# Reordering the second layer of a two-layer image network: next-sample statistics, fractional mix, square roots, final chunks

## The chip, the cores and the metric

The kernel runs on one core of a Trainium2 chip. A core has five engines with a queue of instructions each: TensorE (PE) multiplies matrices from on-chip memory (SBUF) into accumulators (PSUM), VectorE (DVE), ScalarE (ACT) and GpSimd (POOL) work on vectors, and SyncE (SP) issues transfers (DMA). Each engine takes its instructions in the order of its queue and waits at the head of it until the input is there. The metric is the device time of one launch in microseconds (us), lower is better.

## The reference: what is computed

Two residual layers on a batch of 32 images of 96 channels x 56 x 56, each after a group norm over 3 channels:

```python
x = x + L0(_gn(x))      # 1x1 conv to 576 channels, quantise; depthwise 3x3, quantise; 1x1 conv back; + its input
x = x + L1(_gn(x))      # three branches of 32 channels, joined, then a 3x3 conv 96 -> 96

# L1, cut:
x_0, x_05, x_1 = (x[:, :C0], x[:, C0:C - C0], x[:, C - C0:])
x_0 = _group_conv(x_0, conv0_w[None] * Y0[..., None, None], conv0_b, 1)          # spatial branch, gated 3x3
alpha = ALPHA_MIN + (ALPHA_MAX - ALPHA_MIN) * sigmoid(_mlp(gap, ...))[:, 0]      # one angle per sample
Fre = _frft2d(x_05, _frft_mat(H, alpha), _frft_mat(W, alpha))                    # fractional branch
Mix = _group_conv(concat(Fre.real, Fre.imag), conv05_w[None] * Y..., conv05_b, 0)
IFRFT = jnp.abs(_frft2d(Fre_out, _frft_mat(H, -alpha), _frft_mat(W, -alpha))) / (H * W)
...                                                                              # Fourier branch for x_1
out = jnp.concatenate([x_0, IFRFT, x_1], axis=1)
out = conv3x3(out, conv2_w) + conv2_b
```

The gates Y0, Y, Y1 and alpha come from small networks on the channel means of the sample. The absolute value of the fractional branch is a sum of two squares and a square root.

## The kernel before: the parts that the change touches

A sample goes through layer 0 while the sample before it goes through layer 1. Each layer is a list of steps with a weight, and two lists are merged by their weights:

```python
def interleave(a, b):
    ta, tb = sum(c for c, _ in a) or 1, sum(c for c, _ in b) or 1
    ...                               # take from a while (done of a) / ta <= (done of b) / tb

for i in range(B):
    conv, nxt = now["conv"], None
    if i + 1 < B:
        nxt = layer0(i + 1)
        conv[8:8] = nxt["norm"]                       # statistics of the next sample
        at = 2 * (4 * NB - LEAD) + 1                  # NB = 5, LEAD = 7
        conv[at:at] = nxt["split"]                    # its normalised input in two parts
    interleave(conv, one[:-4])                        # one: layer 1 of the sample before
    interleave(now["last"], one[-4:-2])
    head, two, done = layer1(i)
    interleave(head + (nxt["first"] if nxt else []), one[-2:] + end)
    if i + 2 < B:
        load(i + 2)
    one, end, now = two, done, nxt
```

The program's text gives an order of emission; the order of each engine's queue is fixed when the kernel is built, `tile.TileContext(nc, schedule_with_timeline_sim=True)`. Buffers come from pools: `p2` holds two of each tile, `ps1` four PSUM banks, `ps0` two pairs of banks, `xp` three input images.

Layer 0. `expand` (the tiles pe) is the 1x1 convolution to 576 channels of one of four phases of the image; ScalarE and then VectorE quantise it into one of three q1s tiles, and SyncE sends it on to the tiles qp of `depthwise` (pd). `project` (pp) is the last convolution, added into x:

```python
def norm():
    for j in range(NCH):
        nc.vector.bn_stats(stats[:, j, :], xt[:, j * CN : (j + 1) * CN])   # line 333, tile bn
    mean, rstd, _ = group_stats(...)                                       # small matmuls pma, pva
    ...
def expand(b, k):
    ps = pair(...)
    ...                                                                    # 4 matmuls, vh and vl
    src = q1s[turn["q1s"] % 3]
    turn["q1s"] += 1
    quant_act(ps, A1[:, b : b + 1], B1[:, b : b + 1], src[:, :, :PH], ...)
    for g in range(n):
        nc.sync.dma_start(out=qps[(NB * i + b) % 3][...], in_=src[g * G : (g + 1) * G]...)

conv = []
for g in range(NG0):                                  # NG0 = 18
    conv += de[g : g + 1] + ex[LEAD + g : LEAD + g + 1]   # depthwise g, then an expansion
```

Layer 1. After the gates (sg) come `weights` (the gated weights g0, g1, g2), `angles` (cs, and vv by way of pj and pvv), then the branches. `mix_t` (px, tile PQ) and `hilbert` (pr) are the Fourier branch, `spatial` (ps) the first one. The fractional branch mixes its channels, goes through DRAM (z) to be turned, and comes back as zh, with rows of the image in partitions, and az:

```python
def mix_f(j):                                         # j = 0 .. 3
    if j == 0:
        s["z"] = dp.tile([128, 2, HH], F32, tag="z", ...)
    at = slice(HN * j, HN * (j + 1))                  # HN = 392
    for h in range(2):                                # half h of the image: partitions 64 h and on
        t = p2.tile([128, HN], F32, tag="zs", ...)
        rows = slice(LOW * h, LOW * h + G + 2)        # 34 rows
        ps = bank(ps1, f"pm{i}_{j}_{h}")
        nc.tensor.matmul(ps[:, :HN], g1[rows], s["xf"][rows, at], start=True, stop=True)
        if h:
            nc.vector.tensor_copy(t, ps[:, :HN])
        else:
            nc.scalar.copy(t, ps[:, :HN])
        nc.sync.dma_start(out=s["z"][:, h, at], in_=t)
    if j < 3:
        return
    ...                                               # 2 reads z -> zh, then 8 reads z -> az

def rows_f(g):      ...   # g = 0 .. 3: matmuls pi on zh, copies into Y
def columns_f(g):   ...   # g = 0 .. 3: matmuls pz on Y, + az, Square, sum of two -> Z; tile sq has the tag zs

def magnitude():
    dst = cat[G : 2 * G, 1 : 1 + H, 1 : 1 + W].rearrange("p (q r) w -> p q r w", r=4)
    for r in range(4):
        nc.scalar.activation(dst[:, :, r, :], s["Z"][G * r : G * (r + 1)], AF.Sqrt)

def final(j):                                         # j = 0 .. 6: 8 rows of the output each
    ...                                               # 9 matmuls pc on cat, added into x

first = [(0.5, means), (1.0, gates), (0.1, norm)]
steps = [(0.5, weights), (1.0, angles)] + each(1.1, mix_t, 4) + each(1.0, mix_f, 4)
sp = each(2.7, spatial, 2)
steps += sp[:1] + each(2.1, hilbert, 2) + each(1.3, rows_f, 4) + each(1.2, columns_f, 4)
steps += [(0.0, magnitude)] + sp[1:]
steps += each(6.7, final, NCH)                        # NCH = 7
```

`cat` holds the three branches with a border of one element, for the 3x3 convolution. After the last final, `store` writes x out, which frees the image's buffer for `load(i + 2)`.

Of the kernel before, what the change touches and what calls it, by code (L numbers as in the profile page):

```python
# [50 lines left out]
NB = 5  # L51
# [12 lines left out]
LEAD = 7  # L64
L = 57
# [38 lines left out]
def block_kernel(ctx: ExitStack, tc: tile.TileContext, out: bass.AP, a: dict):  # L104
# [8 lines left out]
    p3 = ctx.enter_context(tc.tile_pool(name="p3", bufs=3))  # L113
    dp = ctx.enter_context(tc.tile_pool(name="dp", bufs=2, space=bass.MemoryType.DRAM))
# [138 lines left out]
    for k in range(3):  # L253
        t = cp.tile([128, PH, PW], FP8, tag=f"q1s{k}", name=f"q1s{k}")
        nc.gpsimd.memset(t, 0.0)
        q1s.append(t)
# [68 lines left out]
    def layer0(i):  # L325
# [42 lines left out]
        def expand(b, k):  # L368
# [10 lines left out]
            src = q1s[turn["q1s"] % 3]  # L379
# [70 lines left out]
    def layer1(i):  # L450
# [193 lines left out]
        def mix_f(j):  # L644

            if j == 0:
                s["z"] = dp.tile([128, 2, HH], F32, tag="z", name=f"z{i}")
            at = slice(HN * j, HN * (j + 1))
            for h in range(2):
                t = p2.tile([128, HN], F32, tag="zs", name=f"zs{i}_{j}_{h}")  # L650
                rows = slice(LOW * h, LOW * h + G + 2)
                ps = bank(ps1, f"pm{i}_{j}_{h}")
                nc.tensor.matmul(ps[:, :HN], g1[rows], s["xf"][rows, at], start=True, stop=True)  # L653
                if h:
                    nc.vector.tensor_copy(t, ps[:, :HN])
                else:
                    nc.scalar.copy(t, ps[:, :HN])
                nc.sync.dma_start(out=s["z"][:, h, at], in_=t)
            if j < 3:
                return  # L660
            z = s["z"].rearrange("o u n -> o (u n)")
            for k in range(2):
                nc.sync.dma_start(
                    out=zh[LOW * k : LOW * k + W, :, :W], in_=z[G * k : G * (k + 1)].rearrange("o (h w) -> h o w", w=W)
                )
            az = p1.tile([128, H // 4, 2, W], F32, tag="az", name=f"az{i}")
            s["az"] = az
            for r in range(4):
                for t in range(2):
                    src = z[2 * G + G * t : 3 * G + G * t].rearrange("o (q r w) -> r o q w", r=4, w=W)  # L670
                    nc.sync.dma_start(out=az[G * r : G * (r + 1), :, t, :], in_=src[r])
# [22 lines left out]
        def columns_f(g):  # L694
# [15 lines left out]
            sq = p2.tile([128, 8 * W], F32, tag="zs", name=f"sq{i}_{g}")  # L710
# [6 lines left out]
        def magnitude():  # L717
            dst = cat[G : 2 * G, 1 : 1 + H, 1 : 1 + W].rearrange("p (q r) w -> p q r w", r=4)
            for r in range(4):
                nc.scalar.activation(dst[:, :, r, :], s["Z"][G * r : G * (r + 1)], AF.Sqrt)  # L720
# [252 lines left out]
```

## Time and profile before

| | |
|---|---|
| time, median of 3 runs | 4761.99 us (4741.11 to 4764.95) |
| profiled run | span 4750.5 us, mean granted TensorE clock 0.941 |
| TensorE busy | 4293.0 us, 90% |
| VectorE / ScalarE / GpSimd busy | 2393.3 / 2177.6 / 176.7 us |
| final matmuls pc, line 746 | 1620.7 us |
| depthwise pd, line 398 | 956.8 us |
| expansion pe, line 372 | 434.7 + 351.7 us |
| mix pm, line 653 | 202.7 us, 768 ns mean |
| q1s quantisation waiting for qp transfers | 82.6 us in all |

How to read it: a matmul of float32 data shows as two records, so 16 pm matmul records belong to 8 matmuls of a sample. A bracket after a timeline line tells how long the engine stood idle before it, and which engine, tile and line released it. In a table of stretches the columns are: length, busy time and number of instructions of PE, PEld (the weight load), DVE, ACT, POOL, then the granted TensorE clock (1.00 is full), the DMA engines' share, and GB/s. TensorE counts as busy when it works slowly.

### The profile page before, as it was taken

To read this page: it belongs to the slowest core of one execution; us is meant where nothing else is said; L and a number is where in the kernel's file an instruction comes from. 1 tells how busy PE (TensorE), PEld (TensorE's weight loads), DVE (VectorE), ACT (ScalarE), POOL (GpSimd) and SP (SyncE) were. 2 spreads that over 40 slices of the span, in tenths; PEclk is the share of its full clock that TensorE was granted. 3 is DMA by queue.
4 is the path that set the end of the run, shared out by engine and by line. 5 is a ranking of instruction groups with operands and counts; after the bars stand their busy time and mean duration, and the time that the engine had idled before them with its cause. 6 is when DMAs were issued, how large, how long until landed. Compare 5 with 4: busy or idle time off the path is not lost.

```text
span 4750.5 us, 59888 instructions
## 1 busy us (share of the span) xinstructions
PE 4293.0 (90%) x21632; PEld 2471.1 (52%) x21632; DVE 2393.3 (50%) x5385; ACT 2177.6 (46%) x2824; POOL 176.7 (4%) x209
## 2 busy tenths in 40 slices
PE   3799999999998999999999999999999999999987
PEld 2545555545555555555555555455555555555544
DVE  5545545545445455455454455454454554555532
ACT  3534445444455444455444454444454444554431
POOL 1000000000000000000000000000000000000000
PEclk9899999999999999999999999999999999999998
DMA  2212222211223211222211222122222112222112
GB/s 72 44 48 45 42 61 65 64 46 39 48 62 65 62 38 36 59 64 65 58 40 39 58 65 64 43 42 48 62 65 63 35 39 58 65 64 53 33 34 48
DMA packets 397243, 249.58 MB, mean 53 GB/s; under 512 B 283233, under 2 KB 390100, under 8 KB 390804
## 3 DMA queue, kind: packets, MB, share of 16 engines
q1 hardware_dynamic: 394368, 242.76, 23.0%
q8 instruction: 172, 2.82, 0.3%
q10 hardware_dynamic: 2580, 2.99, 0.2%
q14 instruction: 123, 1.01, 0.1%
HBM read 92.90 MB, written 89.92 MB: 38 GB/s over the span
## 4 chain that ended last, share of the span: by engine, by line
PE 63%; DVE 14%; DMA 11%; ACT 6%; issue 4%; SPq 3%; POOL 0%; DVEq 0%; ACTq 0%; POOLq 0%
PE pc L746 31%; PE pd L398 12%; PE pp L414 5%; DMA zh<-z 4%; PE pe L372 4%; PE pm L653 4%; DMA qp<-q1s 3%; PE pi L678 3%; ACT cat L720 2%; SPq L385 2%; DMA z<-zs 2%; DVE bn L333 2%; DVE q1s L315 2%; DVE x L426 2%; DMA x<-in_x_dram 1%
## 5 line engine op out<-in xcount | busy, mean ns | idle before, releaser
L746 PE MATMUL pc<-cat,wc 96*96 96x448 f32 x4032 | 1620.7, 557 | 60.9 <-ACT cat L720 60.9
L746 PEld LDWEIGHTS pc<-cat,wc 96*96 96x96 f32 x4032 | 664.1, 168 | 895.5 <-issue 809.0
L398 PE MATMUL pd<-qp,dw 128*128 128x392 fp8e4 x4608 | 956.8, 353 | 43.0 <-ACT qtd L313 37.9
L313 ACT ACTIVATE qtd<-pd,o,s 128x784 int16<-128x784 f32 x576 | 576.4, 1001 | 908.1 <-PE pd L398 878.2
L313 ACT ACTIVATE qte<-pe,o,s 128x784 int16<-128x784 f32 x640 | 635.9, 998 | 685.3 <-PE pe L372 669.5
L398 PEld LDWEIGHTS <-dw 128*128 128x128 fp8e4 x4608 | 447.4, 102 | 502.2 <-issue 203.9
L372 PE MATMUL pe<-vh,w1r 96*128 96x392 f32 x1280 | 434.7, 422 | 71.1 <-DVE x L426 41.2
L315 DVE TENSOR_SCALAR q1s<-qte 128x784 fp8e4<-128x784 int16 x640 | 358.8, 562 | 240.4 <-ACT qte L313 144.3
L315 DVE TENSOR_SCALAR q<-qtd 128x784 bf16<-128x784 int16 x576 | 207.0, 359 | 499.1 <-ACT qtd L313 496.4
L754 DVE SCALAR_TENSOR_TENSOR x<-pc,bc,x 96x448 f32<-96x448 f32 x224 | 152.0, 679 | 582.7 <-PE pc L746 581.2
L372 PE MATMUL pe<-vl,w1r 96*128 96x392 f32 x1280 | 351.7, 357 | 0.0
L372 PEld LDWEIGHTS pe<-vh,w1r 96*128 96x128 f32 x1280 | 221.8, 198 | 222.2 <-issue 94.9
L653 PE MATMUL pm<-xf,g 34*128 34x392 f32 x512 | 202.7, 768 | 107.5 <-DVE bn L333 105.0
L414 PE MATMUL pp<-q,w3q 32*96 32x392 bf16 x4608 | 255.8, 327 | 2.2 <-DVE x L426 2.2
L372 PEld LDWEIGHTS pe<-vl,w1r 96*128 96x128 f32 x1280 | 246.1, 198 | 0.5
L426 DVE SCALAR_TENSOR_TENSOR x<-pp,s,x 96x392 f32<-96x392 f32 x256 | 142.2, 616 | 175.8 <-PE pp L414 175.8
L414 PEld LDWEIGHTS <-w3q 32*96 32x96 bf16 x4608 | 182.0, 118 | 84.6 <-issue 31.5
L726 PE MATMUL ps<-xq,g 128*128 128x392 f32 x512 | 201.1, 536 | 0.0
L678 PE MATMUL pi<-cs,zh 120*120 120x112 f32 x1024 | 136.9, 295 | 63.8 <-DMA zh<-z 57.9
L333 DVE BATCH_NORM_STATS2 bn<-x 96x6 f32<-96x448 f32 x224 | 121.1, 608 | 133.6 <-DMA x<-in_x_dram 133.6
L361 ACT CAST vh<-v 96x392 fp32r<-96x392 f32 x256 | 126.2, 516 | 128.7 <-DVE v L353 127.9
L678 PEld LDWEIGHTS pi<-cs,zh 120*120 120x120 f32 x1024 | 131.6, 209 | 75.6 <-DVE cat L640 24.1
(149 smaller groups left out, 3881.5 us busy)
## 6 DMA issues: line engine op xcount, KB each, us to landing
qp<-q1s SPq DMA_DIRECT2D x2304, 26.2 KB
z<-zs SPq DMA_DIRECT2D x256, 196.0 KB
x<-in_x_dram SPq DMA_DIRECT2D x32, 1176.0 KB
out_dram<-x SPq DMA_DIRECT2D x32, 1176.0 KB
zh<-z SPq DMA_DIRECT2D x64, 392.0 KB
az<-z SPq DMA_DIRECT2D x256, 98.0 KB
xf<-vv SPq DMA_DIRECT2D x128, 6.1 KB
prep<-in_w_dram ACTq DMA_DIRECT2D x1, 864.0 KB
```

What stands on the lines that cost most here:

```text
L313: nc.scalar.activation(t.rearrange("p (h n) -> p h n", h=2), ps[:, :, :HN], AF.Relu, bias=offset, scale=scale)
L315: nc.vector.tensor_scalar(dst, src, 15.0, None, ALU.min, saturate=False if dst.dtype == FP8 else None)
L333: nc.vector.bn_stats(stats[:, j, :], xt[:, j * CN : (j + 1) * CN])
L372: nc.tensor.matmul(ps[:, h, :HN], w1[:, 128 * b : 128 * (b + 1)], v[:, k, HN * h : HN * (h + 1)], start=(n == 0), stop=(n == 1),)
L398: nc.tensor.matmul(ps[:, h, :HN], dw[:, g, t, :], view(qps[(NB * i + b) % 3][:, j, :], at, [[PW, PH // 2], [1, PH]]), start=(t == 0), stop ...
L414: nc.tensor.matmul(s["pp"][k // 2][:C, k % 2, :HN], w3[rows, g, :], s["q2"][rows, g, HN * h : HN * (h + 1)], start=(g == 0), stop=(g == NG ...
L426: nc.vector.scalar_tensor_tensor(part, src, A3, part, ALU.mult, ALU.add)
L653: nc.tensor.matmul(ps[:, :HN], g1[rows], s["xf"][rows, at], start=True, stop=True)
L678: nc.tensor.matmul(ps[: LOW + W, 2 * W * k : 2 * W * (k + 1)], zh[:, c : c + 2, :].rearrange("p c w -> p (c w)")[:, : LOW + W], cs, start= ...
L726: nc.tensor.matmul(ps[:, :HN], s["g0"][:, 128 * k : 128 * (k + 1)], view(xq, PH // 2 * h * (W + 2) + k, [[W + 2, PH // 2], [2, PH]]), star ...
L746: nc.tensor.matmul(ps[:C, :CN], wc[:, C * t : C * (t + 1)], cat[:, CR * j + dy : CR * j + dy + CR, dx : dx + W], start=(t == 0), stop=(t = ...
L754: nc.vector.scalar_tensor_tensor(part, ps[:C, :CN], bc, part, ALU.add, ALU.add)
```

## The change

It reorders layer 1 and its seam with layer 0: the next sample's statistics are emitted later; the fractional mix goes by image halves, so that the first half can be read back while the second is mixed, with four staging buffers instead of two; both spatial steps come before the Fourier branch's second part; the square roots are split by rows, so that the first final chunks need only the first part; four final chunks instead of two stand at the border between samples, as work that is ready while the gates are computed; five q1s tiles instead of three.

```diff
+NQ = 5
+HOLD = 4
+    p4 = ctx.enter_context(tc.tile_pool(name="p4", bufs=4))
-    for k in range(3):
+    for k in range(NQ):                              # q1s tiles
-            src = q1s[turn["q1s"] % 3]
+            src = q1s[turn["q1s"] % NQ]
...
-        def mix_f(j):                                # body before: above
+            if j == 0:                               # j = 0 .. 7
+                s["z"] = dp.tile([128, HW], F32, tag="z", name=f"z{i}")
+            h, k = divmod(j, 4)
+            rows = slice(LOW * h, LOW * h + G + 2)
+            ps = bank(ps1, f"pm{i}_{j}")
+            nc.tensor.matmul(ps[:, :HN], g1[rows], s["xf"][rows, HN * k : HN * (k + 1)], start=True, stop=True)
+            t = p4.tile([128, HN], F32, tag="zs", name=f"zs{i}_{j}")
+            if j % 2:
+                nc.vector.tensor_copy(t, ps[:, :HN])
+            else:
+                nc.scalar.copy(t, ps[:, :HN])
+            nc.sync.dma_start(out=s["z"][:, HN * j : HN * (j + 1)], in_=t)
+            if k < 3:
                 return
+            for t in range(2):
+                src = s["z"][G * t : G * (t + 1), HH * h : HH * (h + 1)].rearrange("o (h w) -> h o w", w=W)
+                nc.sync.dma_start(out=zh[LOW * t + PH * h : LOW * t + PH * (h + 1), :, :W], in_=src)
+            if h == 0:
+                return
             ...                                      # the 8 reads of az as before
-            sq = p2.tile([128, 8 * W], F32, tag="zs", name=f"sq{i}_{g}")
+            sq = p4.tile([128, 8 * W], F32, tag="zs", name=f"sq{i}_{g}")
-        def magnitude():
+        def magnitude(h):
+            at = slice(8 * h, min(8 * h + 8, H // 4))
             for r in range(4):
-                nc.scalar.activation(dst[:, :, r, :], s["Z"][G * r : G * (r + 1)], AF.Sqrt)
+                nc.scalar.activation(dst[:, at, r, :], s["Z"][G * r : G * (r + 1), at], AF.Sqrt)
...
-        steps = [(0.5, weights), (1.0, angles)] + each(1.1, mix_t, 4) + each(1.0, mix_f, 4)
-        sp = each(2.7, spatial, 2)
-        steps += sp[:1] + each(2.1, hilbert, 2) + each(1.3, rows_f, 4) + each(1.2, columns_f, 4)
-        steps += [(0.0, magnitude)] + sp[1:]
+        steps = [(1.0, angles), (0.5, weights)] + each(1.1, mix_t, 4) + each(0.6, mix_f, 8)
+        sp, co = each(2.7, spatial, 2), each(1.2, columns_f, 4)
+        steps += sp + each(2.1, hilbert, 2) + each(1.3, rows_f, 4)
+        for h in range(2):
+            steps += co[2 * h : 2 * h + 2] + [(0.1, lambda h=h: magnitude(h))]
         steps += each(6.7, final, NCH)
...
-            conv[8:8] = nxt["norm"]
-            at = 2 * (4 * NB - LEAD) + 1
+            at = 2 * (4 * NB - LEAD)
             conv[at:at] = nxt["split"]
+            conv[at - 6 : at - 6] = nxt["norm"]
-        interleave(conv, one[:-4])
-        interleave(now["last"], one[-4:-2])
+        interleave(conv, one[: -HOLD - 2])
+        interleave(now["last"], one[-HOLD - 2 : -HOLD])
-        interleave(head + (nxt["first"] if nxt else []), one[-2:] + end)
+        interleave(head + (nxt["first"] if nxt else []), one[-HOLD:] + end)
```

More of the change, by code (lines that the diff above doesn't have):

```diff
@@ L646, in mix_f @@
             if j == 0:
[L647 to L659, printed above, removed]
-                return
[L661 to L665, printed above, removed]
+                s["z"] = dp.tile([128, HW], F32, tag="z", name=f"z{i}")
[10 more added lines that the diff above has]
+            if k < 3:
+                return
+            for t in range(2):
[3 more added lines that the diff above has]
+                return
             az = p1.tile([128, H // 4, 2, W], F32, tag="az", name=f"az{i}")
@@ L669, in mix_f @@
                 for t in range(2):
-                    src = z[2 * G + G * t : 3 * G + G * t].rearrange("o (q r w) -> r o q w", r=4, w=W)
+                    src = s["z"][2 * G + G * t : 3 * G + G * t].rearrange("o (q r w) -> r o q w", r=4, w=W)
                     nc.sync.dma_start(out=az[G * r : G * (r + 1), :, t, :], in_=src[r])
```

## The prediction

> **What bounds the kernel now.** I read the page first, then who waits for TensorE's inputs in the steady part (288 to 4467 us, 29 samples of 144.1 us each), then the timeline around the largest wait, then the granted clock stage by stage. The page:
>
> ```profile
> PE 4293.0 (90%) x21632; PEld 2471.1 (52%) x21632; DVE 2393.3 (50%) x5385; ACT 2177.6 (46%) x2824; POOL 176.7 (4%) x209
> ...
> PEclk9899999999999999999999999999999999999998
> ```
>
> TensorE sets the time: 90% busy, the others at half. Only two things can shorten the run without touching the arithmetic: TensorE's idle time, and time at a reduced clock. The waits of TensorE (total us, times, longest) in the steady part:
>
> ```profile
> PE pm L653 <- DVE bn L333: 105.0, 29, 4.3
> PE pc L746 <- ACT cat L720: 48.8, 29, 2.0
> PE pi L678 <- DMA zh<-z: 46.1, 24, 3.9
> PE pe L372 <- DVE x L426: 40.0, 30, 1.3
> PE pmb L295 <- DVE mvb L293: 26.1, 29, 0.9
> PE pd L398 <- ACT qtd L313: 25.6, 58, 0.5
> PE pj L578 <- DVE de L576: 11.4, 29, 0.4
> ```
>
> Per sample (divide by 29): 3.6 us for the next sample's statistics, 1.7 for the square roots, 1.6 for the image read back from DRAM, 1.4 and 0.9 at the border, 0.9 and 0.4 around the angles. The first is the strange one, so the timeline of VectorE and TensorE there:
>
> ```profile
> 2050.99 0.27 DVE L599 COPY vv<-pvv 56x112 f32<-56x112 f32 x1
> 2055.85 3.78 DVE L333 BATCH_NORM_STATS2 bn<-x 96x6 f32<-96x448 f32 x7 [4.59 <-DMA x<-in_x_dram]
> 2059.56 0.73 DVE L622 COPY PQ<-px 112x256 f32<-112x256 f32 x2
> ```
>
> ```profile
> 2055.19 0.52 PE L372 MATMUL pe<-vl,w1r 96*128 96x392 f32 x2
> 2059.69 2.44 PE L653 MATMUL pm<-xf,g 34*128 34x392 f32 x4 [3.98 <-DVE bn L333]
> ```
>
> VectorE stands 4.59 us at a statistics instruction whose input is still being loaded, then spends 3.78 us on it; the copies that free TensorE's PSUM banks stand behind it in the queue. And what follows costs more than the gap (columns: length, busy times, granted clock, DMA share, GB/s):
>
> ```profile
> 2056.00:2060.00 4.00, 0.31 (x1) 0.30 (x2) 4.00 (x9) 0.93 (x2) 0.00 (x0) 1.00 0.03 6
> 2060.00:2067.00 7.00, 7.00 (x18) 2.64 (x17) 3.30 (x9) 1.95 (x3) 0.00 (x0) 0.50 0.26 84
> 2067.00:2074.00 7.00, 7.00 (x21) 2.71 (x20) 1.61 (x4) 2.52 (x4) 0.00 (x0) 0.52 0.38 130
> 2074.00:2088.00 14.00, 11.74 (x71) 8.81 (x71) 7.35 (x20) 8.55 (x12) 0.55 (x1) 1.00 0.74 117
> ```
>
> The 4 us gap is followed by 14 us at half clock. TensorE counts as busy there, so the 90% hides it. The trace holds its own experiment: sample 31 has no next sample, hence no such statistics. The same stretch, from the first matmul after the gates to the first final matmul, for sample 30 and for sample 31:
>
> ```profile
> 4348.30:4416.60 68.30, 57.62 (x312) 38.73 (x310) 35.47 (x93) 39.56 (x57) 0.55 (x1) 0.93 0.46 100
> 4492.30:4552.10 59.80, 52.87 (x297) 36.96 (x295) 29.68 (x75) 37.61 (x55) 0.00 (x0) 0.97 0.43 94
> ```
>
> 68.3 - 59.8 = 8.5 us: that is what a wholly removed statistics stall is worth per sample, gap and slow clock together.
>
> **What the Trainium skill says.** "TensorE: Matmul & The Clock Gate", section "What's actually happening": TensorE's clock falls to half after about one idle window of 3.4 us and comes back after about as much sustained work. The trace agrees on the fall (3.98 us idle, then 0.50); the way back takes 14 us here[...]. The 1.65 us gap before the final matmuls at 2105.83 brings no half clock, so only the largest gap matters for it. "TensorEngine Tiling (Array Packing)", section "Key Properties": tiles on different row groups can load and multiply in parallel. The trace agrees: in the mix (34 rows, at partition 0 and partition 64 in turn) two matmuls of 392 columns take 0.93 us at full clock (sample 31), while the 128-row spatial matmul of 392 columns takes 3.02 / 4 = 0.75 us for one. "ScalarE: Activation LUTs", section "What ACT_TABLE_LOAD costs": about 1283 ns a load; the page's row has 1283 ns, once per sample for Sqrt.
>
> **The change, part by part, per sample.** To place things I laid out the emission order by the weights of the interleaved lists, before and after.
>
> *Statistics later.* They are emitted ahead of the depthwise group 4 in the kernel before, and ahead of group 10, after rows_f(1), in the changed one. Counting TensorE work from the head of layer 1: old place 46 us after the head's start, new place about 84 (7 + 10 expansions at 0.95, 10 depthwise at 1.4, 4 finals at 7.0, the rest some 26). The load lands 44 us after the head's start now (2055.85 - 2011.9). It will land later, at some 54 to 58, because the store that frees its buffer comes after two more finals. In program order the wait would be gone with 26 us to spare. But the trace does not show program order: VectorE reaches bn right after vv, ahead of PQ copies that the program puts earlier, and sample 1's statistics ran at 15.68 us, long before their place. The order is fixed when the kernel is built (schedule_with_timeline_sim), by an estimate of when inputs are ready. So I give the full 8.5 us only half a chance: **-4.2**.
>
> *Mix by image halves, 4 buffers.* The same 8 matmuls, copies (485 and 564 ns) and writes. zh becomes 4 reads of half size instead of 2; the first pair goes out while half two is mixed. Now the chain from the last copy to the first row matmul is 0.57 + 2.66 (write) + 0.4 (issue) + 7.77 (read) = 11.4 us, against 11.2 us of TensorE work emitted between (one spatial, two expansions, two depthwise, hilbert 3.6). After: five expansions 4.7, five depthwise 7.0, two spatial 5.9, hilbert 3.6 = 21.2 us. The wait goes: **-1.6**. The price: matmuls that alternated between row groups now come four times from the same one. Alone each is at most 0.75 us, a pair 1.5 instead of 0.93, so up to 4 x 0.57 = 2.3 us; some neighbours will still overlap: **+1.5**. 4 zs buffers remove waits of the copies for z writes, which are not TensorE's; 5 q1s buffers likewise.
>
> *Square roots in two parts.* Four of 867 ns become four of 448 elements and four of 336. From Square (448: 577 ns, 224: 389) the slope is 0.84 ns an element, so 0.57 and 0.48 us: 4.2 us instead of 3.5 on ScalarE, which has room; the table load stays one. Half of it happens while columns are still computed. Of the 1.7 us wait: **-1.2**.
>
> *Four finals at the border.* The conv list keeps one final instead of three, the head has four instead of two: 14 us more filler between gates and mix_t, where TensorE now waits 0.4 for pj and 0.9 for qtd: **-0.9** of 1.3. The gaps before pe and pmb (2.3 us) lie ahead of the first final that can start; I leave them.
>
> Sum: -4.2 - 1.6 + 1.5 - 1.2 - 0.9 = -6.4 us per sample, x 29 = -186 us: 4762 - 186 = **4575 us**.
>
> **The rivals.** (1) *The stall stays and moves.* bn is again queued at the moment its load is thought to land, now amid mix_f; gap and half clock come back. For it: the two cases of reordering above. Then only -2.2 per sample remains, 64 us: about 4700. (2) *Everything works.* The stall goes wholly, -10.7 per sample, 310 us: about 4450; for it sample 31, and that the DVE has more other work ready at the new place. (3) *The row-group loss and new waits win.* +2.3 for the mix, a conv phase with only one final as ready filler while its chain of small steps is stretched, late loads pushing the statistics and the splits: +1 to +4 per sample, 4790 to 4880. Against it: TensorE's idle share is spread over waits that all get more filler.
>
> **Range and chances.** I weigh (2) at about a third (4420 to 4500), a stall that is shorter and no longer triggers the half clock at a third (4540 to 4660), (1) at a quarter (4670 to 4750), (3) at a tenth. 2% faster is 4667. Eight in ten: 4400 to 4780. Faster by over 2% 0.64, within 2% 0.27, slower 0.09.
>
> **What would show it.** The wait of pm (or any matmul) for bn gone or under 2 us, and mean granted clock up from 0.941 towards 0.97: the first step right; a wait of VectorE for x of 4 us or more: wrong. No wait of pi for zh. The pc wait for cat under 0.6 us. pm's mean up and its busy total per sample over 5 us: the row-group price. A new gap over 3.5 us anywhere, with half clock after it, would make the prediction wrong.

## The result, and the profile after

The changed kernel takes 4922.16 us in the median (4908.78 to 4942.46) against 4760.41 us of the kernel before in the same measurement: a ratio of 1.0351, 95% interval 1.0305 to 1.0398. It is 3.5% slower, where 4575 us and a gain were predicted, and it lies above the predicted range.

Per tile, TensorE's busy and idle time (idle is the time it stood just before the tile), in us of the whole profiled run:

| tile, what it is | before, busy / idle | after, busy / idle |
|---|---|---|
| pm, fractional mix | 202.7 / 107.5 | 244.7 / 106.7 |
| pc, final chunks | 1620.7 / 60.9 | 1706.3 / 82.4 |
| pd, depthwise | 956.8 / 43.0 | 950.9 / 84.6 |
| pe, expansion (vh and vl) | 786.4 / 71.1 | 838.7 / 67.1 |
| pp, projection | 255.8 / 2.2 | 291.7 / 35.3 |
| pi, rows of zh | 136.9 / 63.8 | 120.2 / 0.2 |
| pj, angles | 26.8 / 19.4 | 26.3 / 0.9 |
| TensorE at half clock, sum of the clock records | 566 | 796 |

From the page of the changed kernel, the busy times of its engines and the group of the mix matmuls (busy, mean ns | idle before them, and who ended it):

```profile
PE 4468.9 (91%) x21632; PEld 2622.8 (53%) x21632; DVE 2399.9 (49%) x5385; ACT 2192.9 (45%) x2952; POOL 188.1 (4%) x211
...
L654 PE MATMUL pm<-xf,g 34*128 34x392 f32 x512 | 244.7, 634 | 106.7 <-DMA qp<-q1s 46.8
```

The span grew by 172.7 us (4750.5 to 4923.2), TensorE's busy time by 175.9 for the same 21632 instructions. The idle time did not change (457.5 and 454.3 us); it is the same work that got slower. The mean granted clock fell from 0.941 to 0.919. Half clock grew by 230 us in the records, and half of that, 115 us, is time lost (an estimate from the two sums); the mix matmuls alone are busy 42 us longer. Who makes TensorE wait in the steady part (300 to 4650 us; total us, times, longest):

```profile
PE pc L749 <- ACT cat L723: 73.3, 29, 2.7
PE pd L401 <- ACT qtd L316: 67.7, 58, 1.6
PE pm L654 <- DMA qp<-q1s: 46.8, 13, 4.4
...
PE pm L654 <- DMA xf<-vv: 33.5, 9, 5.0
PE pp L417 <- DVE x L429: 32.0, 29, 1.1
...
PE pm L654 <- issue: 23.5, 7, 3.5
```

The wait of pi for zh is gone from the list, as the change meant. The wait of pm is still there, 103.8 us in three lines under three new names; the wait for the square roots grew from 48.8 to 73.3, that for qtd from 25.6 to 67.7, and the one ahead of the second projection is new. VectorE's own wait at the statistics in that part:

```profile
DVE bn L336 <- DMA x<-in_x_dram: 109.8, 29, 5.1
```

That is 3.8 us per sample: the statistics stand again at the head of VectorE's queue before their input is there. SyncE's issues, and then TensorE and VectorE, around it:

```profile
2132.52 0.83 SPq L606 DMA_DIRECT2D xf<-vv  x1
2133.47 0.79 SPq L133 DMA_DIRECT2D x<-in_x_dram  x1
2134.31 2.40 SPq L606 DMA_DIRECT2D xf<-vv  x3
```

```profile
2141.73 3.78 DVE L336 BATCH_NORM_STATS2 bn<-x 96x6 f32<-96x448 f32 x7 [4.00 <-DMA x<-in_x_dram]
2142.16 4.75 PE L654 MATMUL pm<-xf,g 34*128 34x392 f32 x8 [3.88 <-DMA qp<-q1s]
...
2150.43 2.90 PE L654 MATMUL pm<-xf,g 34*128 34x392 f32 x8
```

The load, 1176 KB, is issued between the four small transfers of vv (6.1 KB each) that the mix reads. It lands at 2141.73, and only then does the mix begin. The mix itself (16 records are 8 matmuls) takes 4.75 + 2.90 = 7.65 us. The stretches after the stall, and after the first final matmul (columns as in the prediction):

```profile
2142.00:2149.00 7.00, 6.84 (x15) 3.06 (x16) 5.54 (x12) 0.97 (x2) 0.00 (x0) 0.57 0.30 96
2149.00:2156.00 7.00, 7.00 (x23) 3.97 (x22) 1.98 (x4) 2.76 (x4) 0.00 (x0) 0.74 0.80 230
...
2186.70:2196.70 10.00, 10.00 (x22) 4.14 (x23) 1.80 (x4) 4.09 (x7) 0.00 (x0) 0.83 0.03 7
```

A stretch of low clock follows the square roots. In the kernel before, that was so in some samples only; two of them, ten microseconds from the first final matmul:

```profile
810.60:820.60 10.00, 9.95 (x22) 4.22 (x23) 8.31 (x18) 6.33 (x11) 0.00 (x0) 0.83 0.02 5
2105.83:2115.83 10.00, 10.00 (x27) 4.46 (x28) 8.98 (x19) 6.60 (x12) 0.00 (x0) 1.00 0.02 5
```

Counted over 28 samples, from the third to the thirtieth, half clock falls into these ten microseconds in 12 of 28 before and in 28 of 28 after. What stands ahead of them in the changed kernel (table load, square roots, first final matmuls):

```profile
2182.98 1.28 ACT L723 ACT_TABLE_LOAD   x1
...
2184.28 2.36 ACT L723 ACTIVATE cat<-Z 32x448 f32<-32x448 f32 x4
...
2186.69 4.16 PE L749 MATMUL pc<-cat,wc 96*96 96x448 f32 x6 [2.53 <-ACT cat L723]
```

The gap is 2.53 us, against 1.65 before, although this part of the square roots is shorter than the undivided ones (2.36 instead of 3.50 us).

### The profile page after: what moved, and what is told of

Read it like the earlier page. It is cut to its first block, busy times and chain, and to the rows that moved or that the text cites. A ratio compares the mean times of both kernels' runs of the same rounds, so it can differ in the third digit from the quotient of the medians.

```text
span 4923.2 us, 59961 instructions
## 1 busy us (share of the span) xinstructions
PE 4468.9 (91%) x21632; PEld 2622.8 (53%) x21632; DVE 2399.9 (49%) x5385; ACT 2192.9 (45%) x2952; POOL 188.1 (4%) x211
## 4 chain that ended last, share of the span: by engine, by line
PE 73%; DVE 14%; ACT 5%; issue 4%; DMA 3%; SPq 1%; POOL 0%; DVEq 0%; ACTq 0%; POOLq 0%
PE pc L749 32%; PE pd L401 12%; PE pe L375 7%; PE pp L417 6%; PE pm L654 5%; PE ps L729 4%; DVE vl L365 2%; DVE x L429 2%; PE px L619 2%; DVE v L356 2%; DVE Y L692 1%; ACT qte L316 1%; DMA xf<-vv 1%; ACT qtd L316 1%; DMA qp<-q1s 1%
## 5 line engine op out<-in xcount | busy, mean ns | idle before, releaser
L749 PE MATMUL pc<-cat,wc 96*96 96x448 f32 x4032 | 1706.3, 582 | 82.4 <-ACT cat L723 82.4
L749 PEld LDWEIGHTS pc<-cat,wc 96*96 96x96 f32 x4032 | 698.1, 176 | 972.1 <-issue 880.0
L401 PE MATMUL pd<-qp,dw 128*128 128x392 fp8e4 x4608 | 950.9, 354 | 84.6 <-ACT qtd L316 79.0
L375 PE MATMUL pe<-vh,w1r 96*128 96x392 f32 x1280 | 463.8, 447 | 67.1 <-DVE x L429 37.1
L375 PE MATMUL pe<-vl,w1r 96*128 96x392 f32 x1280 | 374.9, 377 | 0.0
L654 PE MATMUL pm<-xf,g 34*128 34x392 f32 x512 | 244.7, 634 | 106.7 <-DMA qp<-q1s 46.8
L375 PEld LDWEIGHTS pe<-vh,w1r 96*128 96x128 f32 x1280 | 250.0, 215 | 164.8 <-issue 84.4
L417 PE MATMUL pp<-q,w3q 32*96 32x392 bf16 x4608 | 291.7, 327 | 35.3 <-DVE x L429 35.3
L417 PEld LDWEIGHTS <-w3q 32*96 32x96 bf16 x4608 | 206.2, 117 | 120.2 <-DVE x L429 47.1
L654 PEld LDWEIGHTS pm<-xf,g 34*128 34x128 f32 x512 | 111.1, 228 | 201.7 <-issue 157.0
L336 DVE BATCH_NORM_STATS2 bn<-x 96x6 f32<-96x448 f32 x224 | 121.1, 608 | 120.2 <-DMA x<-in_x_dram 120.2
L741 DVE TENSOR_SCALAR cat<-ps,b 32x392 f32<-32x392 f32 x128 | 79.9, 624 | 139.9 <-ACT cat L743 139.9
```

The lines of the kernel that those rows point to most:

```text
L375: nc.tensor.matmul(ps[:, h, :HN], w1[:, 128 * b : 128 * (b + 1)], v[:, k, HN * h : HN * (h + 1)], start=(n == 0), stop=(n == 1),)
L401: nc.tensor.matmul(ps[:, h, :HN], dw[:, g, t, :], view(qps[(NB * i + b) % 3][:, j, :], at, [[PW, PH // 2], [1, PH]]), start=(t == 0), stop ...
L417: nc.tensor.matmul(s["pp"][k // 2][:C, k % 2, :HN], w3[rows, g, :], s["q2"][rows, g, HN * h : HN * (h + 1)], start=(g == 0), stop=(g == NG ...
L654: nc.tensor.matmul(ps[:, :HN], g1[rows], s["xf"][rows, HN * k : HN * (k + 1)], start=True, stop=True)
L749: nc.tensor.matmul(ps[:C, :CN], wc[:, C * t : C * (t + 1)], cat[:, CR * j + dy : CR * j + dy + CR, dx : dx + W], start=(t == 0), stop=(t = ...
```

## The experiments

Three questions came out of the traces. Why does the mix take so long (theory R: the order of its row groups, made worse by half clock)? What holds the mix, if moving the statistics changes nothing (theory X: the load holds the small transfers)? And what did the new order of steps do (theory S: the split square roots let the final chunks run too early; theory E: the spatial steps come too early)? An earlier theory, T, blamed the four final chunks at the border. Kernels that share a measurement are told together; each ratio is to the kernel before, with its 95% interval. A difference of two ratios is turned into time on 4760 us and carries the errors of both, some 15 to 30 us.

### Theory T: the four final chunks at the border

The changed kernel with two chunks at the border again:

```diff
-HOLD = 4
+HOLD = 2
```

> The changed kernel with two final chunks at the border instead of four (five before the border instead of three), all else of the change kept. Theory T (the tail of layer 0 runs out of final chunks, so the last depthwise groups and the projections stand alone, TensorE falls to half clock for about 10 us after them): 4 to 6 us per sample come back, 4740 to 4810 us, mean granted clock back to about 0.94, the half clock at the head of layer 1 gone. Rival M (the mix by halves, the square roots and the order of the steps cost the time): 4880 to 4930 us, clock still 0.92.

Measured: 5039.97 us, 1.0587 (1.0547 to 1.0627), clock 0.885. And the reverse, the kernel before with four:

```diff
-        interleave(conv, one[:-4])
-        interleave(now["last"], one[-4:-2])
+        interleave(conv, one[:-6])
+        interleave(now["last"], one[-6:-4])
-        interleave(head + (nxt["first"] if nxt else []), one[-2:] + end)
+        interleave(head + (nxt["first"] if nxt else []), one[-4:] + end)
```

> The kernel before with four final chunks at the border instead of two, nothing else of the change. Theory T: nearly the whole loss appears, 4880 to 4980 us, the wait of the second projection for x appears (about 1.1 us per sample) and mean granted clock falls to about 0.92. Rival M: within 1% of before, 4720 to 4800 us.

Measured: 4711.5 us, 0.9897 (0.9863 to 0.9932), clock 0.948. Theory T is wrong in both directions. Four chunks at the border help, by 41 to 49 us on the old kernel and by some 112 on the changed one (ratios 1.0587 and 1.0351, times 4760). The first of these kernels is slower than either theory had it, the second just below the range of rival M. The new gap ahead of the second projection comes with the four chunks in the old kernel (pp idle 34.4, where two had 2.2), but in the changed kernel it stays without them (34.4), so it is not theirs alone.

### Theory R: row groups in turn or one after the other

The changed kernel, with the halves of the image in turn as before, all else as changed:

```diff
-            h, k = divmod(j, 4)
+            k, h = divmod(j, 2)
...
-            nc.sync.dma_start(out=s["z"][:, HN * j : HN * (j + 1)], in_=t)
+            nc.sync.dma_start(out=s["z"][:, HH * h + HN * k : HH * h + HN * (k + 1)], in_=t)
```

> The changed kernel with the eight mix matmuls alternating between the two row groups again (4 staging buffers kept). If matmuls on different row groups overlap: the mix's TensorE time falls from 244.7 to about 203 us, 1.3 us per sample, 4870 to 4890 us in all. If the longer mix was only slow clock: no change, 4905 to 4935 us.

Measured: 4783.39 us, 1.0055 (1.0033 to 1.0077). The order of the mix is 2.96% of 4760, or 141 us of the loss, 4.9 us per sample on 29. The mix of one sample, behind the same stall:

```profile
2082.03 2.11 PE L654 MATMUL pm<-xf,g 34*128 34x392 f32 x8 [3.70 <-DMA xf<-vv]
...
2087.49 1.59 PE L654 MATMUL pm<-xf,g 34*128 34x392 f32 x8
```

2.11 + 1.59 = 3.70 us here, 7.65 in the changed kernel. In the whole run pm is busy 131.4 instead of 244.7 us: 113 of the 141 us lie in the mix matmuls themselves, the rest behind them. The gap ahead is alike, what follows is not: the seven microseconds from 2082.00 have a mean clock of 0.76, those from 2142.00 in the changed kernel had 0.57. The same part alone, put into the kernel before (h outside, the four column parts k inside, nothing else):

```diff
-            at = slice(HN * j, HN * (j + 1))
-            for h in range(2):
+            h = j // 2
+            for u in range(2):
+                k = 2 * (j % 2) + u
+                at = slice(HN * k, HN * (k + 1))
```

> The kernel before with only the order of the eight mix matmuls changed: four on partitions 0 to 33, then four on partitions 64 to 97, two staging buffers and everything else as before. Theory R (alternating row groups overlap, and the mix runs at half clock behind the stall, so that the loss counts double): the mix's TensorE time rises from 202.7 to 300 to 330 us and the run by 90 to 160 us, 4850 to 4915 us. Rival: the order costs only with the rest of the change, under 40 us, 4750 to 4795 us.

Measured: 4869.6 us, 1.025 (1.022 to 1.0281), pm busy 202.7 to 328.7 us. Both directions agree on 115 to 141 us. Whether the price hangs on the stall is told by the pair that has none ahead of the mix, below.

### Theory X: what holds the mix

First, the load earlier by one more image buffer in the kernel before:

```diff
-    xp = ctx.enter_context(tc.tile_pool(name="xp", bufs=3))
+    xp = ctx.enter_context(tc.tile_pool(name="xp", bufs=4))
```

> The kernel before with four buffers for the input image instead of three, so that the load of a sample need not wait for the store of another and lands long before it is used. Theory L (the 1.2 MB load, 8 us long, is what holds up both the statistics on VectorE and the small transfers of vv that the mix waits for): the wait of about 4 us before the mix and the half clock after it go, 7 to 9 us per sample, 4480 to 4560 us, clock above 0.96. Rival S (the stall is the time of the statistics themselves, or another transfer takes its place): 4680 to 4770 us.

Measured: 4920.4 us, 1.0338 (1.0289 to 1.0388). The wait of pm fell from 107.5 to 28.6 us, but the statistics now stand and wait amid the column steps, and the final matmuls' wait for the square roots is 144.1 us; the time lies above both expected ranges. The stall moved to a worse place. So the next kernel keeps the load and holds the statistics back by an operand: a copy into their output tile that needs Y, the tile of the row step.

```diff
+            if i > 1:
+                nc.vector.tensor_copy(view(stats, 0, [[1, 42]]), view(Y[:C], 0, [[1, 42]]))
```

> The changed kernel with alternating mix (4783 us), in which the statistics of the next sample cannot be queued before the row matmuls: a copy of 42 elements of Y into their tile goes first. Theory X (the mix waits for the small transfers of vv, which stand behind the 1.2 MB load in the same queue): TensorE's wait ahead of the mix stays at 3 to 4 us, 4750 to 4800 us. Theory B (it waits for the statistics on VectorE): the wait and the half clock behind it go, 4550 to 4650 us.

Measured, on the kernel with the mix in turn: 4713.99 us, 0.9912 (0.9893 to 0.9931). VectorE waits 10.3 us for x in the whole run, instead of 118.1, and the mix waits as before (104.5 us), released by transfers. Statistics are not what holds it. The time lies below both expected ranges: 68 us less than without the copy, with less half clock (526 instead of 642 us) but a longer wait for the square roots (pc idle 141.5 instead of 82.3); this gain was not taken apart. Two kernels issue the load from GpSimd's queue, without and with that copy:

```diff
-        nc.sync.dma_start(out=xt, in_=x_in[i].rearrange("c h w -> c (h w)"))
+        nc.gpsimd.dma_start(out=xt, in_=x_in[i].rearrange("c h w -> c (h w)"))
```

> The changed kernel with alternating mix, in which the load of x is issued by GpSimd instead of SyncE; the statistics are queued as before. Theory X: the wait ahead of the mix falls under 1.5 us, 4650 to 4730 us. Theory B: it stays at 3 to 4 us, 4770 to 4800 us.

Measured: 4821.02 us, 1.012 (1.0075 to 1.0166); not faster than with the load on SyncE's queue (1.0055, 1.0033 to 1.0077); the intervals just touch.

> Both of the last two edits. Theories X and B agree if each holds half of the stall: the wait ahead of the mix under 0.5 us, mean granted clock 0.96 or more, 4520 to 4620 us. If the load's traffic itself slows the mix's transfers: a wait stays, over 4680 us.

Measured: 4714.77 us, 0.9925 (0.9896 to 0.9954), like the held-back statistics alone. The timeline of this last kernel (SyncE's, GpSimd's and TensorE's lines):

```profile
2037.99 3.28 SPq L608 DMA_DIRECT2D xf<-vv  x4
...
2039.02 0.95 POOL L133 DMA_DIRECT2D x<-in_x_dram  x1 [35.68 <-DVE PQ L627]
...
2047.72 3.13 PE L656 MATMUL pm<-xf,g 34*128 34x392 f32 x8 [3.98 <-DMA qp<-q1s]
```

The four small transfers are issued by 2041.27. The mix starts at 2047.72, on another queue as on the same one. The landing records of the trace (the last update of a transfer's semaphore) tell why: the load landed at 2047.38, the two small transfers issued ahead of it at 2040.02 and 2040.88, the two issued behind it at 2047.59 and 2047.77. Over 26 samples of the changed kernel itself, the small transfer issued ahead of the load takes 2.0 us from issue to landing in the median, the three issued behind it take 6.8. There the statistics end 3.4 us after the mix has begun (median), so they cannot be its wait.

In the kernel before, the load holds the small transfers in another way: SyncE issues the first of them 0.06 us after the load has landed, in all 26 samples, while the copies into vv ended 4.2 us earlier in the median. SyncE's issues in the sample of the prediction, and its wait from 600 to 4200 us:

```profile
2047.24 0.51 SPq L130 DMA_DIRECT2D x<-in_x_dram  x1
...
2055.89 3.26 SPq L603 DMA_DIRECT2D xf<-vv  x4
```

```profile
SPq L603 <- DMA x<-in_x_dram: 74.0, 25, 3.7
```

The mix of that kernel begins 0.06 us after the end of the statistics and 0.14 us after the third small transfer has landed (medians): both hold it for nearly the same time, and while one of them stays, taking away the other gains next to nothing.

Then the load was put where no small transfer waits for it: at the start of the final chunks, ahead of the last steps of layer 0, with a fourth image buffer and a one-element copy that keeps it from being issued earlier. Base is the kernel before with four chunks at the border (4711.5 us):

```diff
+        if i > 2:
+            nc.gpsimd.tensor_copy(xt[G : 2 * G, 0:1], cat[G : 2 * G, H, 1:2])
...
+        if i + 2 < B:
+            load(i + 2)
         interleave(now["last"], one[-6:-4])
...
-        if i + 2 < B:
-            load(i + 2)
```

> The kernel before with four finals at the border (4711 us), with four buffers for x, and with the load of the sample after next moved to the final chunks: one GpSimd copy of an element of cat into the new buffer holds it until the square roots are done, when the DMA engines are idle. Theory X (the load in flight is what the mix's transfers wait for): TensorE's wait ahead of the mix falls under 1 us and with it the half clock behind it, 6 to 8 us per sample, 4460 to 4540 us, clock above 0.965. Rival: the wait moves again (VectorE held by the statistics amid the final chunks), 4650 to 4720 us.

Measured: 4602.52 us, 0.967 (0.9642 to 0.9698), clock 0.963; pm idle 102.4 to 11.9 us, half clock 494 to 344. Theory X holds for the wait: with the load elsewhere the small transfers land 2.0 us after their issue, and the stall is gone. It is worth 2.27% of 4760, 108 us, less than theory X expected (the time lies between the two ranges). The same kernel with the mix by halves:

> The kernel of e9 with the mix by halves of e5. Theory R (a pair of mix matmuls on one row group costs 0.5 us more than on two at full clock, and twice that at half clock): without the half clock the price falls to 1.3 to 2.3 us per sample, 40 to 75 us over e9, instead of 115. If the price has nothing to do with the clock: again 100 to 130 us over e9.

Measured: 4634.08 us, 0.9754 (0.9709 to 0.98). The mix groups of the two pages, first with the halves in turn, then by halves:

```profile
L655 PE MATMUL pm<-xf,g 34*128 34x392 f32 x512 | 174.9, 547 | 11.9 <-issue 4.2
```

```profile
L657 PE MATMUL pm<-xf,g 34*128 34x392 f32 x512 | 220.2, 547 | 13.7 <-DVE PQ L624 4.6
```

220.2 - 174.9 = 45.3 us, 1.4 us per sample, and 40 us of time (0.84% of 4760). Without the stall the row-group order costs 32 to 40 us (the errors of the two ratios allow some 25 more or less), with it 115 to 141: 3 to 4 times as much, not twice. The clock records show one part of it. In the 25 us from the first mix matmul half clock lasts, in the mean of 28 samples, 10.3 us in the kernel before and 19.1 with the mix by halves; 5.2 in the changed kernel with the mix in turn and 10.7 as changed; but 0.2 and 2.3 in the pair without stall. So behind a stall this order not only runs at half clock but makes the half clock last longer. By an estimate, half of the added 5.5 us, 2.7 us, and the 1.4 us of the pair without stall make 4.1 of the 4.9 us per sample. Why the clock comes back later behind one row group is not shown. The load moved in the changed kernel (mix in turn):

> The same move of the load in the changed kernel with alternating mix (4783 us; two staging buffers instead of four, to make room for the fourth x). Theory X: 6 to 8 us per sample less, 4540 to 4600 us. Rival: 4720 to 4790 us.

Measured: 4648.07 us, 0.977 (0.9741 to 0.9799), 136 us below 4783.39, with pm idle at 15.0; again between the two expected ranges.

### Theories S and E: the order of steps

The changed kernel with the mix in turn and the old order after it: one spatial step, Fourier part, rows, columns, square roots in one part, second spatial step.

```diff
-        sp, co = each(2.7, spatial, 2), each(1.2, columns_f, 4)
-        steps += sp + each(2.1, hilbert, 2) + each(1.3, rows_f, 4)
-        for h in range(2):
-            steps += co[2 * h : 2 * h + 2] + [(0.1, lambda h=h: magnitude(h))]
+        sp = each(2.7, spatial, 2)
+        steps += sp[:1] + each(2.1, hilbert, 2) + each(1.3, rows_f, 4) + each(1.2, columns_f, 4)
+        steps += [(0.0, magnitude)] + sp[1:]
```

> The changed kernel with alternating mix, and with the steps after the mix in their old order: the second spatial step after the columns, the square roots in one part. If the new order makes the final chunks come too early and leaves the last depthwise groups and projections without filler, this is what keeps it above the 4711 us of e2: 4700 to 4730 us, the wait of the finals for the square roots back from 2.5 to 1.3 us. If the later statistics or the buffers do it: 4770 to 4800 us.

Measured: 4560.72 us, 0.9569 (0.9513 to 0.9624). I had expected at most half of that. The two halves of this edit apart, first with both spatial steps early and the roots in one part (`steps += sp + ... + [(0.0, magnitude)]`):

> The changed kernel with the mix of before (row groups in turn), both spatial steps early as in the change, but the square roots in one part after all four column steps. The version with all of the old step order took 4561 us, the one with all of the new order 4783. Theory S (splitting the square roots costs: it lets the four final chunks start two pooled tiles earlier, and the end of layer 0 is left without work between its tiles): in the built order the final chunks now start after the 13th of 18 pooled tiles, so 4540 to 4620. Theory E (both spatial steps early cost, because they crowd the time right behind the mix): 4720 to 4800. If each costs about half: 4650 to 4700.

Measured: 4721.82 us, 0.9929 (0.9905 to 0.9953). Then the roots in two parts and the second spatial step behind them, where it was (`steps += sp[:1] + ...`, the loop, `steps += sp[1:]`):

> The opposite half: the second spatial step at its old place after the square roots, but the square roots in two parts as in the change. In the built order the final chunks start half a pooled tile earlier than in the version with all of the old order, and end at nearly the same place. Theory S, in its plain form (the split itself and its second table load are what costs): 4720 to 4800. Theory S in its finer form (not the split, only how early the final chunks run, counts): 4570 to 4650, since they run only a little earlier. Theory E (both spatial steps early cost): 4540 to 4600.

Measured: 4560.53 us, 0.9582 (0.9559 to 0.9606). There is no second table load (32 in the run with the roots in one part or two). Theory E, spatial early, holds: 3.6% of 4760 or 171 us lie in the place of the second spatial step (0.9929 against 0.9569). But the reason is not crowding behind the mix. Two timelines show it: the last columns, the square roots and the first final matmuls, with the second spatial step behind the columns, and then without it.

```profile
2174.21 0.82 PE L704 MATMUL pz<-cs,Y 120*128 120x112 f32 x6
2174.86 3.03 PE L728 MATMUL ps<-xq,g 128*128 128x392 f32 x8
2176.40 1.28 ACT L722 ACT_TABLE_LOAD   x1
2177.70 3.50 ACT L722 ACTIVATE cat<-Z 32x784 f32<-32x784 f32 x4
2177.74 1.54 PE L401 MATMUL pd<-qp,dw 128*128 128x392 fp8e4 x8
...
2181.25 2.12 PE L748 MATMUL pc<-cat,wc 96*96 96x448 f32 x5 [1.27 <-ACT cat L722]
```

```profile
2094.79 0.59 PE L704 MATMUL pz<-cs,Y 120*128 120x112 f32 x4
2098.06 1.28 ACT L722 ACT_TABLE_LOAD   x1
2098.09 1.54 PE L401 MATMUL pd<-qp,dw 128*128 128x392 fp8e4 x8 [0.45 <-ACT qtd L316]
2099.36 3.50 ACT L722 ACTIVATE cat<-Z 32x784 f32<-32x784 f32 x4
2102.91 1.37 PE L748 MATMUL pc<-cat,wc 96*96 96x448 f32 x3 [3.27 <-ACT cat L722]
```

The ten microseconds after the first final matmul, in the same two kernels:

```profile
2181.20:2191.20 10.00, 9.95 (x32) 4.67 (x33) 3.26 (x6) 3.00 (x5) 0.00 (x0) 1.00 0.02 5
```

```profile
2102.90:2112.90 10.00, 9.99 (x23) 4.16 (x23) 2.19 (x5) 1.88 (x2) 0.00 (x0) 0.83 0.02 5
```

The second spatial step, 3.03 us of TensorE that need nothing from the square roots, stood ahead of and under the table load, and so the depthwise tile and the expansion behind it came under the roots. Taken away, the gap grows from 1.27 to 3.27 us and the clock falls behind it: 32 records in ten microseconds against 23. It is so in most samples: half clock in these ten microseconds in none of 28 with the step there, in 22 of 28 without it. In the whole run pc has 1687.0 busy and 108.5 idle instead of 1601.3 and 42.6, so 152 us of the 171 are there. Splitting the roots costs or gains nothing where the spatial step stands behind them, and 60 us where it does not (1.0055 against 0.9929): there the final chunks run earlier still and the last five depthwise tiles stand alone, pd idle 84.2 against 31.1.

The change as it is, with only the old step order put back:

> The change as it is, mix by image halves with one row group four times in a row, with only the old step order put back. Theory R (the row groups cost as long as the stall ahead of the mix leaves TensorE at half clock): the wait of the mix is still there in the version with the mix in turn (104.5 us), so the price is that measured in the other pairs, 115 to 139 us on 4561: 4670 to 4710, slightly faster than the kernel before (4760). If the price belonged to the new step order: 4560 to 4610.

Measured: 4727.89 us, 0.9938 (0.992 to 0.9957). With that one mend the change is 0.6% faster than the kernel before, and the price of its mix order (0.9938 against 0.9569, 176 us, give or take 28) is there as before, rather larger than expected: it does not belong to the new step order.

### Both together, and the staging buffers

The old step order and the load ahead of the last chunks (two staging buffers for want of memory):

> The kernel of 4561 us (changed kernel, mix in turn, old step order) with the load of the sample after next issued ahead of the last chunks of layer 0, as was done before in two kernels, where it took 109 us (4711.5 to 4602.5) and 135 us (4783.4 to 4648.1). If the two costs are separate, 4430 to 4470 and a wait of the mix near 12 to 15 us in place of 104. If the old step order gained because it gives the stretch after the stall its filler, so that both remove the same half clock (412 us of it are left of 642), 4490 to 4550.

Measured: 4547.74 us, 0.9561 (0.9541 to 0.9581): no more than the old step order alone, within the intervals. pm idle fell to 23.5, but pi waits for zh again, 51.7 us. Is that the buffers? The kernel of 4560.72 us with two instead of four, and this one with three (and four q1s tiles):

```diff
-    p4 = ctx.enter_context(tc.tile_pool(name="p4", bufs=4))
+    p4 = ctx.enter_context(tc.tile_pool(name="p4", bufs=2))
```

> The kernel of 4561 us (changed kernel, mix in turn, old step order) with two staging buffers for the mix instead of four. The prediction held that the two extra buffers remove waits that are not TensorE's. If so, 4550 to 4590. Theory B (with two buffers the second half of the mix waits for its writes, the image comes back later, and the wait for it returns): in the built order the first spatial step comes one expansion later behind the mix, the final chunks two pooled tiles later; a wait of the row matmuls of 40 us or more in all, and 4620 to 4680.

Measured: 4570.98 us, 0.9607 (0.9584 to 0.963): the intervals overlap with four buffers; pi idle 25.0 instead of 2.7, and the lost time is won back elsewhere (pp idle 7.5 instead of 34.4).

> The version of 4548 us (old step order, load ahead of the last chunks of layer 0, two staging buffers) with three staging buffers and four quantised tiles instead of five. If the two buffers kept it from gaining what the early load gave elsewhere (109 and 135 us), the wait of the row matmuls for the image falls from 52 us to under 20, and 4430 to 4500. If it is the built order that gives the row matmuls too little between the mix and themselves, and too little half clock was left to gain, the wait stays and 4530 to 4620.

Measured: 4604.32 us, 0.968 (0.9646 to 0.9715), pi idle 59.2, pd idle 63.9: the wait stays, and the kernel is 57 us slower than with two staging buffers. Two things changed in it, the staging buffers and the q1s tiles, so which of them costs this is not shown; but more staging buffers did not bring the gain. In this last kernel the built order has only two depthwise tiles, two expansions, one spatial step and the Fourier part between the last mix matmul and the first row matmul; the wait shows that zh is not there by then. That the early load loses its gain to that wait fits these rows, but is not shown: no run here separates it further.

## Why the prediction was wrong, point by point

**Mix by halves, +1.5 per sample: the mis-sized term.** The working took both matmul durations at full clock, and there it was good: 1.4 us per sample in the pair without stall. But the mix runs directly behind the stall, at 0.57 and 0.74 of the clock, and with this order the half clock lasted twice as long (10.7 us against 5.2). Measured: 4.9 us per sample (141 us). The prediction had shown that stall in its own windows and, by counting on half a chance of its end, priced the mix as if it were gone.

**Square roots in two parts, -1.2: the step that failed most.** It looked at ScalarE's queue (shorter roots, half of them earlier) and not at what TensorE does meanwhile. The second spatial step was the cover; moving it forward was counted as a gain only, as filler for the zh wait. That wait is gone without it too (pi idle 2.7 with the old order). Measured: a loss of about 5.9 us per sample (171 us) for the spatial step, 2.1 (60 us) for splitting on top. Nor did half of the roots run under the columns: in the sample above they begin at 2184.28, and the last column matmuls (2183.57, 0.59 us long) have ended by then. "Only the largest gap matters" was a misreading: the prediction took one sample, at 2105.83, and in 12 of 28 samples of that same trace half clock does follow the 1.65 us gap. After the change it follows in all 28.

**Statistics later, -4.2: wrong, and for a reason that lay a step deeper.** The first half of the doubt was right: the build put the statistics again amid the mix, 4.00 us before their input was there. But the belief that they alone cause the mix's wait was wrong. The wait list named bn since bn's release came last, by less than 0.1 us; the load held the small transfers for the same time. With the statistics out of the way (0.9912) pm idle stayed at 104.5 us. The size was wrong too: the stall wholly removed was worth 108 and 136 us, 3.7 and 4.7 per sample (and within the intervals nothing with the old step order), not 8.5, which was read from the last sample, with 297 TensorE instructions in its stretch instead of 312.

**zh wait, -1.6: right in the number, not by the reasons given.** 63.8 us idle became 0.2, but it is also down to 2.7 with the mix in turn and the old step order, where neither the halves nor the early spatial step can have done it; two staging buffers instead of four there bring 25.0. **Four chunks at the border, -0.9: right in sign, too small,** 41 to 49 us or 1.4 to 1.7 per sample on the old kernel. **Buffers, no effect: right** for the time, within the intervals, though not for the waits.

**The sum.** By ratios, the change consists of -205 us (everything but the three items that follow, the 0.9569 of the kernel with the old order), +171 (second spatial step early), +60 (roots split on top of it), +141 (mix order): -205 + 171 + 60 + 141 = +167, which is the 3.51% measured on 4760. (Half an interval is 26 us for the first item, so for the second about 28.) Being a chain of ratios, it adds up whatever the parts are, and the shares depend on the order: splitting the roots costs nothing with the spatial step behind them, and the mix order costs 176 us with the old step order. For what is in the -205 the prediction had -4.2 - 1.6 - 0.9 = -6.7 per sample, -194 us; that this is near is luck, since the stall that was to give the 4.2 is still there (pm idle 104.5). 41 to 49 of the 205 is the chunks at the border, pi idle fell by 61 and pj by 18, and the rest (the later statistics, the five q1s tiles, the angles ahead of the weights) was not taken apart. Of the rivals, the third (row groups and new waits win) is what came, with 42 us more than its upper end, and had been given one chance in ten; the first (the stall stays) came with it.

## What to carry to other kernels

Price an added cost at the clock of the place where it will stand, not at full clock: behind the stall the same order of the mix cost 3 to 4 times what it cost without. Before a step is moved forward as filler for one wait, ask which wait it covers now; here the place of 3 us of matmul per sample was worth 171 us. Read a stretch of the trace in many samples before a rule is taken from it: one sample showed no half clock where 12 of 28 had it. And when a wait is blamed on the instruction that ended last, look which transfers were in flight beside it, then take away one cause at a time.

## What the runs showed of the hardware

The large load held small transfers whatever queue issued it. On one queue (the changed kernel, 26 samples) 6.1 KB transfers landed 2.0 us after their issue when issued ahead of the 1176 KB load, and 6.8 us when issued behind it (medians); with the load on GpSimd's queue the figures were 2.0 and 7.3. The Trainium skill says in "DMA: Bandwidth & Descriptors", section "Issuing engines are not separate DMA queues", that transfers run on the same 16 engines and interleave, whoever issued them. The delay from another queue agrees with shared engines; but here the small transfers did not get through in between as a whole.

Half clock followed gaps well below the window of about 3.4 us that "TensorE: Matmul & The Clock Gate", section "What's actually happening", gives for the fall. Of 28 samples each, half clock came in the ten microseconds after the square-root gap in none where the gap was 1.27 us (old step order, mix in turn), in 12 where it was 1.65 (before), in 28 where it was 2.52 (changed), and in 22 where it was 3.27 (both spatial steps early, roots in one part): it is not the length of that gap alone that decides. The stretches of half clock in the records last nearly all a multiple of about 3.4 us, up to 20.5 in the changed kernel and 23.9 in the one before, with one odd stretch in each.
